# A graph kernel's attention: the row of s_dst through a DRAM line instead of TensorE transposes

## The chip, the cores and the metric

The kernel runs on one core of one Trainium2 chip. The metric is device time in microseconds (us), the median of the runs of a kernel. A profiled span is about 2 us shorter than the timed run (1584.6 against 1587.04 us before).

## The reference, cut to what matters

`x` is 64 x 256 x 128: 64 graphs of 256 nodes, 128 features each, all with one adjacency matrix. Four layers follow one another: a recurrent one (five steps), a masked graph convolution, an attention layer with an MLP, and a Chebyshev convolution. The change touches only the scores of the third layer.

```python
def _L2_gnn_ref(x, A_final, Wp, bp, a_src, a_dst, ...):
    h = jnp.einsum('bmi,ih->bmh', x, Wp) + bp
    s_src = jnp.einsum('bmh,h->bm', h, a_src)
    s_dst = jnp.einsum('bmh,h->bm', h, a_dst)
    scores = s_src[:, :, None] + s_dst[:, None, :]     # s_dst is needed as a row
    scores = jnp.where(scores >= 0, scores, 0.2 * scores)
    scores = jnp.where((A_final <= 0)[None], fill, scores)
    attn = jax.nn.softmax(scores, axis=-1)
    weighted_adj = attn * A_final[None]
    h_gat = jnp.einsum('bmn,bnh->bmh', weighted_adj, h)
    # ... layer norm, MLP, residual
```

## The kernel before

The batch is worked off as 32 pairs of graphs, each pair as four tiles of 128 tokens. Many pairs are in flight at once. A list scheduler inside the program decides, before anything runs, the order in which each engine's instructions stand. The scheduler plans with the costs that each `add` states, with one latency per engine (`SP` is the queue that issues nearly all transfers, 1383 of 1385), and with a place rule that says how far apart the pairs start.

```python
LATENCY = {PE: 230, ACT: 80, DVE: 80, POOL: 120, SP: 1800}

def place(p):
    return 20000 * min(p, 28)
# ... (cut)
        def turn(src, dst, view=lambda b: b.ap, tiles=4):    # transpose through DVE and 4 transfers
            S = flat("S") if tiles == 4 else big("S8")
            add(DVE, 705 if tiles == 4 else 1240,
                lambda: nc.vector.transpose(...), [src], [S], [S])
            def f():
                for k in range(4):
                    nc.sync.dma_start(dst.ap[:, :, 32 * k:32 * k + 32],
                                      S.ap[32 * k:32 * k + 32].rearrange("s (y r) -> s y r", r=32))
            add(SP, 2730, f, [S], [dst], [dst])
            return dst
# ... (cut) a recurrent step: mix (matmuls on htok), gates, the new state, and then
            h = turn(hT, wide("htok"))
# ... (cut) the attention; h2 holds h, s_src (column D) and s_dst (column D + 1)
        ts, sd = bank(), flat("sd")
        def f():
            for c in range(4):
                nc.tensor.transpose(ts.ap[:, c * P:(c + 1) * P],
                                    h2.ap[:, c, D + 1:D + 2].to_broadcast([P, P]), ident.ap)
        add(PE, 450, f, [h2, ident], [ts], [ts, sd])
        add(ACT, 585, lambda: nc.scalar.copy(sd.ap.rearrange("p (c x s) -> p c x s", x=4, s=32),
                                             ts.ap.rearrange("p (c s x) -> p c x s", x=4, s=32)), [ts], [sd])
# ... (cut) VectorE adds the mask to sd (tile u), softmax, turn(u) -> wT, matmul of wT with h
```

`htok` is the state of a pair by token: the result of each recurrent step, and the input of the next step's `mix`, brought to TensorE by four transfers of 64 KB on the SyncE queue.

## Time and profile before

| | before |
|---|---|
| time, median of the runs beside the changed kernel | 1587.35 us |
| span of the profiled execution | 1584.6 us |
| TensorE stream, summed from the matmul records | 1514.3 us |
| lost on TensorE: 100 to 1400 us / after 1400 us | under 7 us / 49.7 us |
| one pair, from its first matmul on wT to the next pair's | 47.1 us |

The stream is the sum of the distances from one matmul record to the next, each counted as at most the usual distance for its shape. "Lost" is time in which TensorE stands idle or runs at a lowered clock. First the windows view over the long middle; its columns are start and end, length, then busy us and instructions of TensorE, its weight loads, VectorE, ScalarE, GpSimd, then the granted clock, the DMA share and GB/s:

```profile
100.00:1400.00 1300.00, 1298.67 (x5384) 895.54 (x5384) 934.76 (x2059) 836.62 (x1883) 370.33 (x398) 1.00 0.44 77
```

TensorE is idle for 1300 - 1298.67 = 1.3 us in 1300. Second, the end of the view of the tile htok, how long its 640 transfers take from issue to landing:

```profile
DMA to landing us min/median/max: 2.3/2.4/3.9
```

They land in 2.4 us, none later than 3.9.

### The profile page before, as it was taken

The page shows a single profiled execution, that of the slowest core. Times are in us where ns is not written, and L with a number is a line of the kernel's source. Part 1 is how long each engine was busy: PE and PEld are TensorE (multiplying, and loading weights), DVE is VectorE, ACT ScalarE, POOL GpSimd, SP SyncE. Part 2 cuts the span into 40 slices and gives each one's busy share as a digit, 9 for nine tenths or more (in the row PEclk, how much of TensorE's full clock was granted, in tenths as well). Part 3 has the DMA queues.
Part 4 walks back from the last instruction along what each step waited for, and adds up shares of the span by engine and source line. Part 5 has one row for each costly group of instructions (what it writes and reads, how often), then busy time and mean ns, then how long its engine had stood idle before and what let it go on. Part 6 is the DMA issues. An engine that isn't in the chain of part 4 may idle for free.

```text
span 1584.6 us, 21441 instructions
## 1 busy us (share of the span) xinstructions
PE 1538.7 (97%) x6382; PEld 1070.4 (68%) x6382; DVE 1104.4 (70%) x2465; ACT 992.1 (63%) x2245; POOL 441.5 (28%) x487
## 2 busy tenths in 40 slices
PE   8999999999999999999999999999999999998767
PEld 5556667666677676667676667766767766676656
DVE  4687787667767677767676867776776766677553
ACT  3355676666666666666666666656666666677554
POOL 0001233332222323223323232233232231244441
PEclk9999999999999999999999999999999999999788
DMA  6223444444443444443444444344444344334422
GB/s 204 45 36 52 67 66 84 73 87 84 75 84 74 72 81 87 76 84 74 74 79 87 76 80 79 71 77 87 78 77 85 70 72 88 62 70 68 79 54 60
DMA packets 756611, 121.98 MB, mean 77 GB/s; under 512 B 743184, under 2 KB 743184, under 8 KB 756496
## 3 DMA queue, kind: packets, MB, share of 16 engines
q1 hardware_dynamic: 756208, 120.09, 42.1%
q8 instruction: 52, 0.85, 0.2%
q14 instruction: 63, 0.52, 0.1%
q10 hardware_dynamic: 288, 0.53, 0.1%
HBM read 19.86 MB, written 8.39 MB: 18 GB/s over the span
## 4 chain that ended last, share of the span: by engine, by line
PE 91%; DVE 2%; DMA 2%; ACT 2%; SPq 1%; issue 1%; POOL 1%; POOLq 0%; ACTq 0%; DVEq 0%
PE ps L513 27%; PE ps L607 9%; PE ps L589 9%; PE ps L597 8%; PE ps L605 8%; PE ps L592 8%; PE ps L740 7%; PE ps L526 6%; PE ps L702 4%; PE ps L749 3%; PE ps L647 2%; SPq L498 1%; PE ps L658 1%; DMA wT<-S 1%; DMA hT<-xT_in 1%
## 5 line engine op out<-in xcount | busy, mean ns | idle before, releaser
L516 ACT COPY mix<-ps 128x512 f32<-128x512 f32 x256 | 148.1, 580 | 197.7 <-PE ps L513 196.5
L513 PE MATMUL ps<-aTs,htok 128*128 128x256 f32 x1024 | 242.4, 380 | 2.8 <-DMA htok<-S 2.6
L513 PEld LDWEIGHTS ps<-aTs,htok 128*128 128x128 f32 x1024 | 192.6, 190 | 69.6 <-issue 32.8
L569 POOL TENSOR_SCALAR ss<-ss 128x4 f32<-128x4 f32 x96 | 38.2, 398 | 603.0 <-DVE ss L562 601.7
L611 DVE TENSOR_TENSOR hv<-hv,hT 128x512 f32<-128x512 f32 x160 | 124.2, 777 | 98.8 <-ACT hv L609 97.3
L570 POOL TENSOR_TENSOR rs<-ss,neg_half 128x4 f32<-128x4 f32 x128 | 139.2, 1087 | 192.0 <-DVE ss L564 183.8
L602 DVE SCALAR_TENSOR_TENSOR tr<-tr,hT 128x512 f32<-128x512 f32 x160 | 118.4, 742 | 91.4 <-ACT tr L595 91.3
L607 PE MATMUL ps<-tr,u5h 128*128 128x512 f32 x320 | 163.6, 594 | 0.4 <-DVE tr L602 0.2
L589 PE MATMUL ps<-hT,W 128*128 128x512 f32 x320 | 162.4, 593 | 1.1 <-DMA hT<-xT_in 1.1
L592 PE MATMUL ps<-mix,w4s 128*128 128x512 f32 x320 | 162.9, 593 | 0.0
L597 PE MATMUL ps<-mix,dw 128*128 128x512 f32 x320 | 162.8, 593 | 0.0
L605 PE MATMUL ps<-mix,w5s 128*128 128x512 f32 x320 | 162.6, 593 | 0.0
L609 ACT ACTIVATE hv<-ps,bh 128x512 f32<-128x512 f32 x160 | 109.4, 685 | 83.2 <-PE ps L607 80.6
L600 ACT ACTIVATE tz<-ps,bz 128x512 f32<-128x512 f32 x160 | 109.4, 685 | 60.0 <-PE ps L597 58.6
L595 ACT ACTIVATE tr<-ps,br 128x512 f32<-128x512 f32 x160 | 108.4, 679 | 39.3 <-PE ps L592 39.0
L612 DVE SCALAR_TENSOR_TENSOR hv<-tz,hv 128x512 f32<-128x512 f32 x160 | 108.9, 694 | 24.0 <-ACT tz L600 22.6
L562 DVE TENSOR_REDUCE ss<-sq 128x4 f32<-128x512 f32 x128 | 87.1, 681 | 48.1 <-ACT sq L559 48.1
L492 DVE STREAM_TRANSPOSE S<-hT 128x512 f32<-128x512 f32 x160 | 112.3, 703 | 1.1
L614 DVE SCALAR_TENSOR_TENSOR hT<-hv,hT 128x512 f32<-128x512 f32 x160 | 108.8, 693 | 4.9
L607 PEld LDWEIGHTS ps<-tr,u5h 128*128 128x128 f32 x320 | 60.4, 190 | 50.4 <-issue 36.4
L605 PEld LDWEIGHTS ps<-mix,w5s 128*128 128x128 f32 x320 | 58.6, 191 | 51.5 <-issue 31.1
L589 PEld LDWEIGHTS ps<-hT,W 128*128 128x128 f32 x320 | 58.3, 190 | 49.1 <-issue 42.8
(174 smaller groups left out, 2904.2 us busy)
## 6 DMA issues: line engine op xcount, KB each, us to landing
htok<-S SPq DMA_DIRECT2D x640, 64.0 KB, 2.4
xT<-S SPq DMA_DIRECT2D x256, 64.0 KB, 2.4
wT<-S SPq DMA_DIRECT2D x128, 128.0 KB, 3.8
xs<-xs_in SPq DMA_DIRECT2D x32, 256.0 KB, 2.8
hT<-xT_in SPq DMA_DIRECT2D x32, 256.0 KB, 3.0
dT<-S SPq DMA_DIRECT2D x128, 64.0 KB, 2.3
zT<-S SPq DMA_DIRECT2D x128, 64.0 KB, 2.4
y_out<-o SPq DMA_DIRECT2D x32, 256.0 KB, 2.0
```

The lines of the kernel that those rows point to most:

```text
L492: lambda: nc.vector.transpose(S.ap.rearrange("p (x c r) -> p x c r", x=4, c=tiles), view(src).rearrange("p (c x s) -> p x c s", x=4, c=til ...
L513: nc.tensor.matmul(t.ap[:, b * N:(b + 1) * N], src.ap[:, 2 * b + j, :], m.ap[:, j, :], start=(j == 0), stop=(j == 1))
L516: add(ACT, 590, lambda: nc.scalar.copy(o.ap, t.ap), [t], [o])
L570: nc.gpsimd.tensor_tensor(rs.ap, ss.ap, neg_half.ap, op=ALU.pow)
L589: add(PE, 865, lambda tg=tg: nc.tensor.matmul(tg.ap, mat("u3"), hT.ap, start=True, stop=False, skip_group_check=True), [hT, W0], [tg], [tg ...
L592: add(PE, 865, lambda tg=tg, mT=mT: nc.tensor.matmul(tg.ap, w4s.ap, mT.ap, start=False, stop=False, skip_group_check=True), [mT, w4s], [tg])
L597: add(PE, 865, lambda tg=tg, mT=mT: nc.tensor.matmul(tg.ap, dw.ap, mT.ap, start=False, stop=True, skip_group_check=True), [mT, dw], [tg])
L602: add(DVE, 735, lambda tr=tr: nc.vector.scalar_tensor_tensor(tr.ap, tr.ap, 1.0, hT.ap, op0=ALU.add, op1=ALU.mult), [hT], [tr])
L605: add(PE, 865, lambda tv=tv, mT=mT: nc.tensor.matmul(tv.ap, w5s.ap, mT.ap, start=True, stop=False), [mT, w5s], [tv], [tv, hv])
L607: add(PE, 865, lambda tv=tv, tr=tr: nc.tensor.matmul(tv.ap, u5h.ap, tr.ap, start=False, stop=True), [tr, u5h], [tv])
L611: add(DVE, 735, lambda hv=hv: nc.vector.tensor_sub(hv.ap, hv.ap, hT.ap), [hT], [hv])
L740: nc.tensor.matmul(tt[i].ap[:, b * N:(b + 1) * N], s, w.ap.rearrange("p k d -> p (k d)"), start=(b == 0 and k == 0), stop=False, skip_grou ...
```

## The change

Its intent is to take work from the busiest engine. Four transposes per pair leave TensorE and one copy leaves ScalarE. Instead, column D + 1 of h2 is written to a 2 KB line in DRAM (512 pieces of 4 bytes), and the line is read back into all 128 partitions. The row now has another order of nodes, so the mask addition, the transposing copy (`run=64`) and the order of one adjacency matrix follow it. The place rule changes too.

```diff
 def place(p):
-    return 20000 * min(p, 28)
+    return 24000 * min(p, 29)
@@ attention
-        ts, sd = bank(), flat("sd")
-        def f():
-            for c in range(4):
-                nc.tensor.transpose(ts.ap[:, c * P:(c + 1) * P], h2.ap[:, c, D + 1:D + 2].to_broadcast([P, P]), ident.ap)
-        add(PE, 450, f, [h2, ident], [ts], [ts, sd])
-        add(ACT, 585, lambda: nc.scalar.copy(...), [ts], [sd])
+        line, sd = Buf("line", 8, lambda i: dram.tile([1, 512], F32, tag=f"line{i}", name="line")), flat("sd")
+        add(SP, 650, lambda: nc.sync.dma_start(line.ap.rearrange("o (q s) -> s q o", s=32), h2.ap[:, :, D + 1:D + 2]),
+            [h2], [line], [line])
+        add(SP, 430, lambda: nc.sync.dma_start(sd.ap, line.ap.to_broadcast([P, 512])), [line], [sd], [sd])
@@ cut: mask addition on [p, 4, 64] views, turn(u, ..., run=64), host order of adjacency "as"
```

More of the change, by code (lines that the diff above doesn't have):

```diff
@@ L162 @@
     work = ctx.enter_context(tc.tile_pool(name="work", bufs=1))
+    dram = ctx.enter_context(tc.tile_pool(name="dram", bufs=1, space=bass.MemoryType.DRAM))
     psum = ctx.enter_context(tc.tile_pool(name="psum", bufs=1, space=bass.MemoryType.PSUM))
@@ L486, in add, with turn @@
             g.add(eng, cost, fn, (p, n[0]), reads, writes, takes)
-        def turn(src, dst, view=lambda b: b.ap, tiles=4):
+        def turn(src, dst, view=lambda b: b.ap, tiles=4, run=32):
             S = flat("S") if tiles == 4 else big("S8")
             add(DVE, 705 if tiles == 4 else 1240,
-                lambda: nc.vector.transpose(S.ap.rearrange("p (x c r) -> p x c r", x=4, c=tiles),
-                                            view(src).rearrange("p (c x s) -> p x c s", x=4, c=tiles)),
+                lambda: nc.vector.transpose(S.ap.rearrange("p (x c r) -> p x c r", x=4, r=run),
+                                            view(src).rearrange("p (c x s) -> p x c s", x=4, s=run)),
                 [src], [S], [S])
@@ L652, in build @@
                 hbias.ap[:, None, :].to_broadcast([P, 2, HW])), [t2, hbias], [h2])
-        ts, sd = bank(), flat("sd")
-        def f():
-            for c in range(4):
-                nc.tensor.transpose(ts.ap[:, c * P:(c + 1) * P], h2.ap[:, c, D + 1:D + 2].to_broadcast([P, P]), ident.ap)
-        add(PE, 450, f, [h2, ident], [ts], [ts, sd])
-        add(ACT, 585, lambda: nc.scalar.copy(sd.ap.rearrange("p (c x s) -> p c x s", x=4, s=32),
-                                             ts.ap.rearrange("p (c s x) -> p c x s", x=4, s=32)), [ts], [sd])
+        line, sd = Buf("line", 8, lambda i: dram.tile([1, 512], F32, tag=f"line{i}", name="line")), flat("sd")
+        add(SP, 650, lambda: nc.sync.dma_start(line.ap.rearrange("o (q s) -> s q o", s=32), h2.ap[:, :, D + 1:D + 2]),
+            [h2], [line], [line])
+        add(SP, 430, lambda: nc.sync.dma_start(sd.ap, line.ap.to_broadcast([P, 512])), [line], [sd], [sd])
         u = big("u")
@@ L671, in f @@
                 nc.vector.tensor_tensor_reduce(
-                    out=uc(c), in0=sd.ap[:, b * N:(b + 1) * N], in1=maskb.ap[:, it, :], scale=1.0,
+                    out=uc(c).rearrange("p (x f) -> p x f", x=4), in0=sd.ap.rearrange("p (x f) -> p x f", x=4)[:, :, 64 * b:64 * b + 64], in1=maskb.ap[:, it, :].rearrange("p (x f) -> p x f", x=4), scale=1.0,
                     scalar=-3.4e38, op0=ALU.add, op1=ALU.max, accum_out=mx.ap[:, c:c + 1])
@@ L692, in build @@
             a_s.ap.rearrange("p t j -> p (t j)")[:, None, :].to_broadcast([P, 2, 512])), [a_s], [u])
-        wT = turn(u, temp([P, 8, P], "w", N_W, "wT"), tiles=8)
+        wT = turn(u, temp([P, 8, P], "w", N_W, "wT"), tiles=8, run=64)
         add(DVE, 160, lambda: nc.vector.scalar_tensor_tensor(rd.ap, rd.ap, LN_EPS, rd.ap, op0=ALU.mult, op1=ALU.mult),
@@ L790 @@
     rows = [L1_gnn_bias, L2_gnn_bp, L2_gnn_gat_g, L2_gnn_gat_b, L2_gnn_b1, L2_gnn_b2, e[0, N - 1:], L2_gnn_eps]
-    adjs = {"a": adj, "as": adj[nodes], "ass": adj[nodes][:, nodes], "aTs": adj.T[nodes],
+    adjs = {"a": adj, "as": adj[nodes].reshape(N, 2, 4, 32).transpose(0, 2, 1, 3).reshape(N, N), "ass": adj[nodes][:, nodes], "aTs": adj.T[nodes],
             "aTss": adj.T[nodes][:, nodes]}
```

## The prediction

> **What bounds the kernel now.** I read the page's first two parts (busy shares, the 40 slices), then the chain of waits, then the busy time by window, then the groups of the lines that the change removes, then the timeline of one attention.
>
> ```profile
> PE 1538.7 (97%) x6382; PEld 1070.4 (68%) x6382; DVE 1104.4 (70%) x2465; ACT 992.1 (63%) x2245; POOL 441.5 (28%) x487
> ...
> PE   8999999999999999999999999999999999998767
> ...
> PEclk9999999999999999999999999999999999999788
> ...
> PE 91%; DVE 2%; DMA 2%; ACT 2%; SPq 1%; issue 1%; POOL 1%; POOLq 0%; ACTq 0%; DVEq 0%
> ```
>
> TensorE is busy to the nines until four slices from the end, and the chain that ended last is 91% TensorE. The other engines have a quarter or more of the span free. By window (length, then busy us and instructions of PE, PEld, DVE, ACT, POOL, then granted clock, DMA share, GB/s):
>
> ```profile
> 800.00:1000.00 200.00, 200.00 (x830) 137.87 (x829) 143.81 (x311) 132.37 (x302) 59.90 (x64) 1.00 0.45 78
> 1400.00:1450.00 50.00, 47.97 (x250) 37.34 (x249) 37.60 (x85) 38.02 (x96) 20.82 (x24) 1.00 0.47 78
> 1450.00:1500.00 50.00, 36.35 (x186) 30.49 (x184) 32.90 (x88) 34.40 (x93) 20.35 (x22) 0.86 0.44 69
> 1500.00:1550.00 50.00, 35.75 (x156) 30.22 (x157) 27.88 (x79) 29.12 (x76) 23.10 (x29) 0.80 0.29 51
> ```
>
> So there are two regimes. Up to about 1400 us TensorE never stops and its own stream sets the pace; the same attention matmul comes at 813.89, 861.03 and 908.17 us, one pair of the batch every 47.1 us, 32 pairs in all. After 1400 us the last pairs run out of company: TensorE waits, the granted clock falls to 0.80, and the length of one pair's chain of dependent work sets the end. From the starts of the matmul records I get 1514 us of pure streaming, about 6 us before the first matmul, 4 us of small gaps in the first 200 us, 1.5 us at 1318 us, 50 us lost after 1400 us (idle and slow clock) and 8 us after the last matmul: 1584 us. A timed run is about 2.4 us longer than the span (1587.04 against 1584.6).
>
> The removed part, over the whole run and in one pair:
>
> ```profile
> L658 PE MATMUL ps<-ident,h x128: 272/273/273, 139.6 to 1511.3; 128*128 128x128 f32 x128
> ...
> L660 ACT COPY sd<-ps x32: 579/586/592, 140.4 to 1511.6; 128x512 f32<-128x512 f32 x32
> ```
> ```profile
> 874.91 0.60 PE L658 MATMUL ps<-ident,h 128*128 128x128 f32 x4
> 875.54 0.59 ACT L660 COPY sd<-ps 128x512 f32<-128x512 f32 x1 [2.78 <-PE ps L658]
> 876.16 0.43 DVE L671 CUSTOM_DVE_ANT_0 u<-sd,maskb 128x256 f32<-128x256 f32 x1 [0.32 <-ACT sd L660]
> 892.65 3.61 SPq L498 DMA_DIRECT2D wT<-S  x4
> 908.17 1.95 PE L702 MATMUL ps<-h,wT 128*128 128x128 f32 x16
> ```
>
> A transpose's record lasts 273 ns, but that is latency: four start within 0.33 us, 0.11 us apart, and the chain puts 0.44 us on the four. The last wT transfer of this pair landed at 899.2 us and its matmul began at 908.2, so 9 us of waiting in the queue lie between the attention weights' arrival and their use.
>
> [...] The new write takes column D+1 of h2, so 512 elements of 4 B; the htok transfers of before also have 512 pieces (of 128 B), and land in 2.4 us. No transfer of before has 4-byte pieces. [...] here the y_out store lands 2.0 us after issue, so a DRAM target shows no penalty. [...] granted 1.00 while TensorE is full, 0.80 in the gappy tail. [...]
>
> **The change part by part.**
> Removed: 32 x 4 transposes x 0.111 us = 14.2 us of TensorE stream, 0.9% of the span. In the first regime all of it is on the path: a pair should take 47.14 - 0.44 = 46.7 us. Also 32 ACT copies x 0.586 = 18.8 us, on an engine 63% busy, so worth nothing there, and one use of a PSUM bank per pair.
> Added: 64 DMAs on the SyncE queue. Its 1280 transposing issues at 0.63 us (wT 0.79) take about 830 us, and it waits some 600 us, so another 64 x about 0.65 = 42 us fit. In the program's order four htok issues stand between the line's write and its read in nearly every pair of the first regime: 4 x 0.63 = 2.5 us, about the landing time of the write, so the read should block that in-order queue by a microsecond at most.
> The path of one pair: out go 0.44 (transposes) + 0.02 + 0.59 (copy), about 1.1 us. In come 0.65 issue + 2.4 landing (as htok) + 0.6 issue + 2.8 landing (as xs, also 256 KB out of DRAM) = 6.4 us, less about 0.8 because issues and landings overlap as they are counted. Net +4.5 us per attention.
> Moved: s_dst's order inside the row changes, and with it runs of 64 instead of 32 in the transposing copy and in the mask addition; element counts stay, so I count 0. The place rule (24000, 29 instead of 20000, 28) reorders everything. I listed both orders and summed the matmul streams between a pair's own matmuls. From h2's last matmul to the first one on wT: 36.1 us before, 39.0 after; the extra 3 us pay most of the 4.5, so some 7 us of the 9 remain and the detour is hidden. Elsewhere the new order is tighter (a pair lives 327 us of stream instead of 366), but the smallest distances, 12 us from the attention's matmul to the next mix and 14.7 us from u5h to the next mix, still exceed what those chains need in the trace (about 7.5 and 9.5 us).
> The tail: behind the last pair's first matmul stand 159 us of matmuls before and 179 after; behind the last matmul of its fifth recurrent step, 70 and 90. That last pair took from 1462.4 to 1577 us in the trace, 114.6 us for 70 us of stream: bound by its own chain. In the new order the same matmul should come at about 1421 x 0.992 (the streams I summed are 0.8% over the measured ones) + 6 + 4 + 1.5 + 5 of early tail gaps = 1427 us. Then 114.6 + 4.5 for the DRAM detour + 0 to 10, because now three pairs (not two) arrive there within 2 us of each other and queue for DVE, ACT and SyncE: last matmul at 1546 to 1556, span 1554 to 1564, timed 1556 to 1567.
> Sum: 14.2 us from the stream, about 12 us from a better filled tail: **1561 us**, 1.6% less.
>
> **The rivals.**
> (a) Only the stream counts and the tail loses its 50 us as before: 1587 - 14 = 1573. For: tail losses are stubborn, and the three pairs in step compete. Against: the last pair starts with 20 us more work behind it.
> (b) The SyncE queue becomes the bound: slow 4-byte writes (say 5 us) block it and htok comes late to matmuls in a fixed order. A stall of 1 us per pair would cost 32 us and give 1590. Against: the page's wait for DMA in the first regime is near 0, the distance at the attention is 39 us, and the recurrent steps have 5 us to spare.
> (c) The tail fills almost fully: streams 1500 + 6 + 4 + 2 + about 25 + 8 = 1545 span, 1548 timed. For: 114 - 90 = 25 us is the least that the last pair's chain leaves idle. Against: it needs no contention at all.
> (d) DMA load: 16384 pieces of 4 B are 2% more packets at a DMA share of 0.45; nothing.
>
> **Range and chances.** The first term is sure to a microsecond or two; the tail term may be -3 to +30. I take 1547 to 1576 for 8 in 10. Faster by over 2% means under 1555.3 us: 0.26. Slower by over 2% needs (b) in full: 0.03. Within 2%: 0.71.
>
> **What would show it.** The pair period in the middle 46.7 us and TensorE 200 of 200 us there; no L658 and L660 group; ACT's copy time down 19 us; the line's write landing in 2 to 3 us and sd's read in about 3; SyncE's wait on the line of a microsecond per pair; the matmul on wT not waiting for DMA before 1400 us; and the tail's loss after the last pair's fifth step about 35 us instead of 45. Wrong would be: TensorE gaps before 1300 us behind htok or wT, a landing of the line over 5 us, or a tail as long as before.

## The result, and the profile after

The changed kernel is correct, and slower.

| | before | after |
|---|---|---|
| time, median (range, runs) | 1587.35 us (1585.71 to 1587.93, 4) | 1687.38 us (1682.29 to 1695.21, 4) |
| span of the profiled execution | 1584.6 us | 1686.2 us |
| TensorE stream | 1514.3 us | 1500.3 us |
| TensorE idle, 100 to 1400 us | 1.3 us | 54.6 us |
| one pair in the middle | 47.1 us | 48.6 to 51.6 us |

The ratio is 1.0636, with a 95% interval of 1.0594 to 1.0678. Ratios here are the mean time of one kernel's fast runs over that of the other's fast runs of the same rounds, so they are not quite the ratio of the medians.

The stream fell by 14.0 us, close to the 14.2 predicted (13.3 if the usual distances are taken from the kernel before for both). The time rose by 100 us. First the page of the changed kernel: busy shares, slices, and the chain that ended last, by engine and by line.

```profile
PE 1555.9 (92%) x6254; PEld 1066.3 (63%) x6254; DVE 1127.9 (67%) x2465; ACT 983.6 (58%) x2213; POOL 426.9 (25%) x487
...
PE   8999999999999999999999999999999999996566
...
PE 63%; DMA 14%; DVE 13%; SPq 4%; issue 3%; ACT 2%; POOL 1%; ACTq 0%; DVEq 0%; POOLq 0%
PE ps L514 16%; DMA htok<-S 6%; PE ps L590 6%; PE ps L593 6%; PE ps L527 6%; PE ps L737 6%; PE ps L608 5%; PE ps L598 5%; PE ps L606 5%; SPq L499 4%; DMA line<-h 4%; PE ps L699 3%; PE ps L746 3%; DVE hv L613 3%; DMA sd<-line 2%
```

The slices still show nines, because a loss of 4% does not move a digit. The chain shows it at once: TensorE's share fell from 91% to 63%, DMA and VectorE took 27%. The largest transfer in it is not one of the two new ones but htok, which the change did not touch. The windows view, as before, has the middle and the end:

```profile
100.00:1400.00 1300.00, 1245.45 (x5027) 847.80 (x5026) 905.45 (x1950) 792.96 (x1780) 340.27 (x381) 0.99 0.47 78
...
800.00:1000.00 200.00, 192.42 (x790) 132.01 (x789) 138.72 (x299) 122.65 (x277) 54.15 (x61) 0.99 0.47 80
...
1500.00:1550.00 50.00, 34.26 (x150) 25.53 (x149) 30.23 (x84) 29.93 (x76) 16.64 (x19) 0.87 0.38 63
1550.00:1600.00 50.00, 31.81 (x154) 27.27 (x153) 24.93 (x69) 22.39 (x62) 11.96 (x16) 0.79 0.42 71
1600.00:1650.00 50.00, 30.04 (x162) 25.26 (x161) 26.19 (x55) 28.42 (x79) 24.30 (x28) 0.90 0.38 64
```

The stretch that was full (200.00 of 200) now has 192.42, and the other 200 us stretches from 200 to 1400 us have 189.72 to 193.30. Next, the transfers (KB each, median us to landing), and then the last line of the view of htok:

```profile
htok<-S SPq DMA_DIRECT2D x640, 64.0 KB, 2.4
...
sd<-line SPq DMA_DIRECT2D x32, 256.0 KB, 4.0
...
line<-h SPq DMA_DIRECT2D x32, 2.0 KB, 6.9
```
```profile
DMA to landing us min/median/max: 2.3/2.4/8.2
```

The write of 2 KB takes 6.9 us, longer than the 64 to 256 KB transfers of the steady state (medians of 2.3 to 4.0 us). The median of htok is unchanged, which hides what its maximum shows: 8.2 us instead of 3.9. I sorted the records: the 113 htok transfers issued within 4.5 us after a line write landed in a median of 6.0 us, the other 527 in 2.36. The waits view has who paid (us in total, times, longest us), first of the changed kernel:

```profile
DVE u L668 <- DMA sd<-line: 147.9, 31, 7.0
...
PE ps L514 <- DMA htok<-S: 43.6, 31, 2.9
```
```profile
SPq L658 <- DMA line<-h: 105.0, 30, 6.8
```

and then the one of them that the kernel before has too:

```profile
PE ps L513 <- DMA htok<-S: 2.6, 2, 1.3
```

There are three waits, each about once per pair: VectorE for the row, TensorE for htok, and SyncE's queue for the line. The timeline of SyncE's queue (start us, duration) shows one pair:

```profile
763.08 0.62 SPq L656 DMA_DIRECT2D line<-h  x1
763.79 2.66 SPq L499 DMA_DIRECT2D htok<-S  x4
769.38 0.33 SPq L658 DMA_DIRECT2D sd<-line  x1
```

The order is the one that the prediction counted on: write, four htok, read. The line landed at 769.32, and the four htok, issued between 763.79 and 765.82, landed at 769.49, 769.66, 769.83 and 771.48: the first three within half a microsecond after the line, none before it. The chain of waits, in order of time, shows what that did to TensorE in this pair and in the next:

```profile
765.82 5.66 DMA htok<-S
...
771.57 2.66 PE ps L514 x8
774.23 1.71 PE ps L590 x2
775.94 1.87 PE ps L514 x8
...
816.16 6.84 DMA htok<-S
...
823.14 3.03 PE ps L514 x8
```

The htok transfer lies on the chain with 5.66 us. TensorE stood for 2.06 us at 771.57. Then it was slow: eight mix matmuls took 2.66 us (1.73 elsewhere in the same chain), the next two 1.71 (0.86 elsewhere). The windows view in short stretches says why:

```profile
771.50:772.50 1.00, 0.93 (x4) 0.87 (x5) 0.00 (x0) 0.00 (x0) 0.00 (x0) 1.00 1.15 155
772.50:773.50 1.00, 1.00 (x4) 0.85 (x3) 0.00 (x0) 0.00 (x0) 0.00 (x0) 0.60 0.82 159
773.50:774.50 1.00, 1.00 (x3) 0.69 (x3) 0.71 (x5) 0.24 (x1) 0.00 (x0) 0.50 1.08 167
774.50:776.00 1.50, 1.50 (x3) 0.60 (x2) 1.43 (x9) 1.50 (x5) 0.00 (x0) 0.50 0.63 104
```

The granted clock fell to one half at 772.69 us for 3.41 us, 1.1 us after the end of the stall of 2.06 us. In the clock records of the changed kernel it did so nine times between 100 and 1400 us, for 3.41 us each, during a stall of TensorE or within 1.4 us after one; those nine stalls were 2.06 to 3.00 us long. One of 2.17 us (573.16 to 575.33) and all under 2 us left the clock at 1.00; why that one did, was not shown. So a stall that the waits view counts as 2.06 us costs about 2.06 + 0.93 + 0.85 + 0.14 = 4.0 us, most of the difference between the 46.7 us that were promised for a pair and the 51.1 that this one took. Over 100 to 1400 us the clock took 15.4 us in this way (the granted clock of 260 stretches of 5 us, summed), beside the 54.6 us of idleness: 70 us in the middle. In the kernel before, not one of those stretches was below 1.00. After 1400 us the changed kernel lost 86 us on TensorE, against 49.7 before, and that is most of the rest of the 100 us.

### The profile page after: what moved, and what is told of

It reads as the page before. It is cut to its first block, busy times and chain, and to the rows that moved or that the text cites. A ratio compares the mean times of both kernels' runs of the same rounds, so it can differ in the third digit from the quotient of the medians.

```text
span 1686.2 us, 21327 instructions
## 1 busy us (share of the span) xinstructions
PE 1555.9 (92%) x6254; PEld 1066.3 (63%) x6254; DVE 1127.9 (67%) x2465; ACT 983.6 (58%) x2213; POOL 426.9 (25%) x487
## 4 chain that ended last, share of the span: by engine, by line
PE 63%; DMA 14%; DVE 13%; SPq 4%; issue 3%; ACT 2%; POOL 1%; ACTq 0%; DVEq 0%; POOLq 0%
PE ps L514 16%; DMA htok<-S 6%; PE ps L590 6%; PE ps L593 6%; PE ps L527 6%; PE ps L737 6%; PE ps L608 5%; PE ps L598 5%; PE ps L606 5%; SPq L499 4%; DMA line<-h 4%; PE ps L699 3%; PE ps L746 3%; DVE hv L613 3%; DMA sd<-line 2%
## 5 line engine op out<-in xcount | busy, mean ns | idle before, releaser
L514 PE MATMUL ps<-aTs,htok 128*128 128x256 f32 x1024 | 252.3, 391 | 44.4 <-DMA htok<-S 43.6
L570 POOL TENSOR_SCALAR ss<-ss 128x4 f32<-128x4 f32 x96 | 21.1, 220 | 926.7 <-DVE ss L563 887.5
L612 DVE TENSOR_TENSOR hv<-hv,hT 128x512 f32<-128x512 f32 x160 | 110.3, 690 | 125.7 <-ACT hv L610 125.6
L590 PE MATMUL ps<-hT,W 128*128 128x512 f32 x320 | 165.8, 603 | 3.0 <-DMA hT<-xT_in 2.7
L571 POOL TENSOR_TENSOR rs<-ss,neg_half 128x4 f32<-128x4 f32 x128 | 133.2, 1041 | 69.7 <-DVE ss L565 45.9
L613 DVE SCALAR_TENSOR_TENSOR hv<-tz,hv 128x512 f32<-128x512 f32 x160 | 136.9, 857 | 20.7 <-ACT tz L601 19.2
L668 DVE CUSTOM_DVE_ANT_0 u<-sd,maskb 128x256 f32<-128x256 f32 x128 | 46.8, 422 | 147.9 <-DMA sd<-line 147.9
L603 DVE SCALAR_TENSOR_TENSOR tr<-tr,hT 128x512 f32<-128x512 f32 x160 | 108.5, 679 | 23.7 <-ACT tr L596 23.2
L678 ACT ACTIVATE u<-u,h 128x256 f32<-128x256 f32 x128 | 54.5, 496 | 100.0 <-DVE mx L668 100.0
```

The source lines that it names most:

```text
L514: nc.tensor.matmul(t.ap[:, b * N:(b + 1) * N], src.ap[:, 2 * b + j, :], m.ap[:, j, :], start=(j == 0), stop=(j == 1))
L571: nc.gpsimd.tensor_tensor(rs.ap, ss.ap, neg_half.ap, op=ALU.pow)
L590: add(PE, 865, lambda tg=tg: nc.tensor.matmul(tg.ap, mat("u3"), hT.ap, start=True, stop=False, skip_group_check=True), [hT, W0], [tg], [tg ...
L612: add(DVE, 735, lambda hv=hv: nc.vector.tensor_sub(hv.ap, hv.ap, hT.ap), [hT], [hv])
L613: add(DVE, 735, lambda hv=hv, tz=tz: nc.vector.scalar_tensor_tensor(hv.ap, tz.ap, 1.0, hv.ap, op0=ALU.add, op1=ALU.mult), [tz], [hv])
```

## The experiments

At hand were these theories. **Hold**: the write delays the completion of the transfers behind it. **Standing queue**: SyncE stands at the read until the line has landed, and everything behind it in the queue is issued late. **Late row**: VectorE stands at the mask addition for the row. **Order**: the new place rule is worse by itself. And for the write itself: is it slow for its number of pieces, their scattered order, their size, or its target?

All kernels, with what each left on TensorE in the middle. Idle is 1300 us less the busy time from 100 to 1400 us. W: values wrong. (1): one run only, state unknown.

| label | kernel | time us | ratio to before (95%) | idle us |
|---|---|---|---|---|
| | before | 1587 | 1 | 1.3 |
| | changed | 1687.4 | 1.0636 (1.0594 to 1.0678) | 54.6 |
| e3_no_write | W no write, row from a constant | 1593.6 | 1.0038 (1.0021 to 1.0054) | 2.9 |
| e4_write_not_read | W write, row from a constant | 1682.4 | 1.0588 (1.0568 to 1.0608) | 51.9 |
| e8_dve_no_wait | W all transfers, VectorE reads a constant | 1663.9 | 1.0499 (1.0468 to 1.0529) | 51.5 |
| e17_nobody_waits | W e4 and e8 together | 1648.8 | 1.0394 (1.0376 to 1.0412) | 43.7 |
| e18_write_from_act | W e4, write on ScalarE's queue | 1651.8 | 1.0417 (1.0398 to 1.0435) | 45.4 |
| e12_4B_to_sbuf | W e4, 512 x 4 B into SBUF | 1593.6 | 1.0040 (1.0023 to 1.0056) | 4.0 |
| e11_4B_in_order | 512 x 4 B in order of partitions | 1764.5 | 1.1113 (1.1094 to 1.1131) | 89.3 |
| e14_128_of_4B | W e4, 128 x 4 B | 1632.2 (1) | | 27.1 |
| e20_128_of_8B | W e4, 128 x 8 B | 1600.2 (1) | | 8.3 |
| e5_16B | 128 x 16 B | 1635.6 | 1.0288 (1.0266 to 1.0310) | 26.0 |
| e1_place_only | before, new place rule | 1608.8 | 1.0132 (1.0117 to 1.0147) | 5.3 |
| e2_old_place | changed, old place rule | 1776.3 | 1.1185 (1.1164 to 1.1206) | 105.8 |
| e15_dve_no_wait_old_place | W e8, old place rule | 1630.5 | 1.0271 (1.0254 to 1.0288) | 33.7 |
| e16_no_write_old_place | W e3, old place rule | 1619.3 | 1.0218 (1.0188 to 1.0248) | 29.6 |
| e7_latency | changed, scheduler told | 1619.9 | 1.0211 (1.0192 to 1.0230) | 23.4 |
| e10_16B_told | 16 B, told, old place rule | 1699.0 | 1.0702 (1.0686 to 1.0717) | 65.4 |
| e13_16B_replanned | 16 B, told, a third place rule | **1578.1** | 0.9945 (0.9930 to 0.9960) | 0.9 |

### Which part of the change costs the time

**e3_no_write.** The write is left out, and the row is read from a constant in DRAM of the same size. The order of the instructions is kept.

```diff
-        add(SP, 650, lambda: nc.sync.dma_start(line.ap.rearrange(...), h2.ap[:, :, D + 1:D + 2]), [h2], [line], [line])
-        add(SP, 430, lambda: nc.sync.dma_start(sd.ap, line.ap.to_broadcast([P, 512])), [line], [sd], [sd])
+        add(SP, 650, lambda: None, [h2], [line], [line])
+        add(SP, 430, lambda: nc.sync.dma_start(sd.ap, <512 constants of rows, to all partitions>), [line], [sd], [sd])
```

> The changed kernel with the write of the line left out and the row read from a constant input in DRAM (wrong values on purpose); every engine's order is that of the changed kernel. Theory A: the middle is full again, a pair every 46.7 us, and the time comes to 1555 to 1575 us. Theory B or theory C (the 256 KB read into every partition, or the load of the DMA rings): stays at 1660 us or more.

Measured: 1593.6 us, 94 us less than the changed kernel. In the middle the losses are gone (windows view):

```profile
100.00:1400.00 1300.00, 1297.08 (x5325) 890.72 (x5324) 959.71 (x2051) 841.66 (x1880) 362.27 (x402) 1.00 0.46 82
```

One pair takes 46.705 us, the 46.7 of the prediction. So the removal did what was promised, and reading 256 KB per pair, the strided VectorE forms and the new order cost the middle nothing. But the time is 33 us above the predicted 1561. It lies at the end: the last pair's fifth step came at 1430.0 us (predicted 1427), and from there the last matmul was 151.3 us away instead of the predicted 119 to 129. That second error is taken up under e1_place_only.

**e4_write_not_read.** The write is kept and the row comes from the constant, so SyncE does not stand at the read.

```diff
-        add(SP, 430, lambda: nc.sync.dma_start(sd.ap, line.ap.to_broadcast([P, 512])), [line], [sd], [sd])
+        add(SP, 430, lambda: nc.sync.dma_start(sd.ap, <512 constants of rows, to all partitions>), [line], [sd], [sd])
```

> The changed kernel with the write kept but the row read from a constant input, so that nothing waits for the write's landing (wrong values on purpose, same order). If the harm is only that SyncE and VectorE wait for the landing: as without the write, 1555 to 1575 us. If the write also holds up the transfers issued behind it (htok issued within 4.5 us after it landed in 6.0 us in place of 2.4): a good part of the loss stays, 1600 to 1650 us, and htok behind the write still lands in about 6 us.

Measured: 1682.4 us, only 5 less than the changed kernel and 89 more than without the write. Nobody uses what is written, and it still costs. Its transfers, in the order of that view:

```profile
sd<-rows_in SPq DMA_DIRECT2D x32, 256.0 KB, 5.5
...
line<-h SPq DMA_DIRECT2D x32, 2.0 KB, 7.1
```

The time is above both branches of the expectation. The htok transfers right behind a write landed in 6.2 us, though SyncE issued them without standing: line 749.42 to 756.09, htok issued from 750.14 on and landed at 756.26, 756.44, 756.61, 757.78. The read of the constant row, which has nothing to do with the line, takes 5.5 us instead of the 3.7 of e3_no_write, and VectorE waits 96.6 us for it instead of 37.2. The queue standing at the read falls as the main cause, the hold stands. (SyncE still waited 23.5 us in all for the line, before transfers that do not use it, L499. In the changed kernel's trace SyncE's 1447 issues share 8 semaphores, so a semaphore that is used again is the likely reason.)

**e8_dve_no_wait** and **e17_nobody_waits.** In the first all transfers are as changed, but VectorE adds the mask to a constant that is always there. The second does that and takes the row from the constant as well, so neither SyncE's read nor VectorE depends on the line.

```diff
-                    in0=sd.ap.rearrange(...)[:, :, 64 * b:64 * b + 64],
+                    in0=rbc.ap[:, :512].rearrange(...)[:, :, 64 * b:64 * b + 64],
```

> The changed kernel with both transfers and every order kept, but VectorE's addition reads a constant tile in place of the row (wrong values on purpose), so that no engine but SyncE waits for the row. If the loss goes through transfers held up behind the write (htok landing in 6 us): stays at 1670 us or more. If it goes mainly through VectorE standing still for the row (148 us in the trace): falls to 1600 to 1640 us.

> The changed kernel with the 4-byte write and a read of a constant row both issued, and nobody waiting for either (wrong values on purpose, same order). What is left above the 1594 us without a write is the hold on the transfers behind the write: 1640 to 1665 us if that is the main cause, below 1615 us if the waits for line and row are.

Measured: 1663.9 and 1648.8 us. With e3_no_write that makes a stair, each step a difference of medians: 1593.6 without the write; + 55.2 for a write that nobody waits for; + 15.1 when SyncE stands at the read; + 23.5 when VectorE waits for the row as well: 1687.4. In the other order, through e4_write_not_read, the last two steps are 33.6 for VectorE and 5.0 for SyncE, so those two cannot be parted sharply. The first step is the largest in either order. (1663.9 lies between the two branches of its expectation; 1648.8 is inside its first one.) The 33.6 us of VectorE in e4 belong to the hold as well: the row that VectorE waits for there is a constant, and e3, where it waits for the same constant, is the base of the stair. So 55 us is what the hold costs with nobody at the row, and 89 us what it costs with nobody needing the line. One limit: in e17 SyncE still waited 17.1 us for the line at the same place, L499, so "nobody waits" is not quite literal.

**e18_write_from_act.** As e4, but the write is issued on ScalarE's queue, while htok stays on SyncE's.

```diff
-        add(SP, 650, lambda: nc.sync.dma_start(line.ap.rearrange(...), h2.ap[:, :, D + 1:D + 2]), [h2], [line], [line])
+        add(SP, 650, lambda: nc.scalar.dma_start(line.ap.rearrange(...), h2.ap[:, :, D + 1:D + 2]), [h2], [line], [line])
```

> The kernel in which nothing reads the write (1682 us), with the write issued from ScalarE's queue in place of SyncE's. If the hold is in SyncE's own queue: htok issued within 4.5 us after the write lands in 2.4 us again and the time falls to 1590 to 1605 us. If it is in the DMA engines, across queues: htok behind it still takes about 6 us and the time stays at 1660 us or more.

Measured: 1651.8 us, between the two branches and 31 us below e4. The transfers view names the other queue:

```profile
line<-h ACTq DMA_DIRECT2D x32, 2.0 KB, 6.6
```

SyncE's waits for the line fell to 1.9 us in all, and htok behind a write still took 6.0 us. So the hold is not the order of one queue: a write of 6.6 us on ScalarE's queue holds htok on SyncE's. Where it sits was not shown. The semaphore records of the changed kernel show how closely the quick transfers follow the slow one. Each of these landings is counted in 16 steps; those of the line shown above came from 766.28 to 769.32 us, and those of the first htok behind it from 766.46 to 769.49, each 0.16 to 0.21 us after the line's. But it is not the notice alone that is late. In the records of the single pieces, 169 pieces of 128 bytes took over 1 us each between 100 and 1400 us of the changed kernel, the longest 3.3 us; in the kernel before, e3_no_write, e12_4B_to_sbuf, e20_128_of_8B and e5_16B not one took over 0.3 us. So part of the data of the quick transfers is held too. (The 31 us below e4 go with having the write off SyncE's queue; how, was not traced.)

### What makes the write slow

**e12_4B_to_sbuf.** As e4, but the same 512 pieces of 4 bytes go into an SBUF tile.

```diff
-        line, sd = Buf("line", 8, lambda i: dram.tile([1, 512], ...)), flat("sd")
+        line, sd = temp([P, 4, 2], "line", 8), flat("sd")
-        add(SP, 650, lambda: nc.sync.dma_start(line.ap.rearrange(...), h2.ap[:, :, D + 1:D + 2]), ...)
+        add(SP, 650, lambda: nc.sync.dma_start(line.ap[:, :, 0:1], h2.ap[:, :, D + 1:D + 2]), ...)
```

> As the experiment in which nothing reads the write (1682 us), but the 512 pieces of 4 B go to SBUF, each to its own partition, in place of DRAM (wrong values on purpose, same order). If 4 B pieces into DRAM are the cause: landing about 2.4 us, htok behind it no later than elsewhere, 1585 to 1600 us. If 4 B pieces are slow wherever they go: 1670 us or more.

Measured: 1593.6 us, exactly as without the write, and its line in the transfers view is:

```profile
line<-h SPq DMA_DIRECT2D x32, 2.0 KB, 2.0
```

Pieces, issues and queue are those of e4, and all 89 us are gone. The DRAM target is needed for the harm (landing in 7.1 us, here 2.0). It also clears the 32 extra issues of 0.6 us.

**e11_4B_in_order.** The pieces go to DRAM in the order of the partitions, 16 adjoining bytes from each, rather than scattered; a ScalarE copy sorts the row after the read.

```diff
-        ... line.ap.rearrange("o (q s) -> s q o", s=32) ...
+        ... line.ap.rearrange("o (p c) -> p c o", c=4) ...
+        add(ACT, 585, lambda: nc.scalar.copy(<sd in order>, <raw>), [raw], [sd])
```

> As the 16 B experiment (ScalarE puts the row in order), but without the gathering: 512 pieces of 4 B again, written to the line in the order of the partitions[...]. If the cost goes by the number of pieces: the landing stays at 6 to 7 us and the time is 1680 us or more. If it is the scattering over one another's DRAM lines: the landing falls to 2 to 3 us and the time to the 1636 us of the 16 B kernel, give or take 10.

Measured: 1764.5 us, values right; the write lands in 7.4 us, htok behind it in 6.2. The scattered order is not the cause. (The time suffers from the added copy in an order planned for none, so only the landing is used.)

**e14_128_of_4B** and **e20_128_of_8B.** As e4 with fewer pieces: 128 of 4 bytes (one of the four columns), or 128 of 8 bytes, gathered first by a VectorE copy.

```diff
# e14
+        ... line.ap.rearrange("o (c s x) -> s x c o", x=4, c=4)[:, :, 0, :], h2.ap[:, 0, D + 1:D + 2] ...
# e20
+        add(DVE, 160, lambda: nc.vector.tensor_copy(dcl.ap, h2.ap[:, :, D + 1]), [h2], [dcl], [dcl])
+        ... line.ap.rearrange("o (p c) -> p (o c)", c=4)[:, 0:2], dcl.ap[:, 0:2] ...
```

> As the experiment in which nothing reads the write, but only one of the four columns is written: 128 pieces of 4 B in place of 512 (wrong values on purpose). If the landing goes by the number of pieces put into DRAM: about 1.8 to 2.3 us, as with 128 pieces of 16 B, and the kernel at 1585 to 1605 us. If it is the size of 4 B: 6 us or more and over 1660 us.

> 128 pieces of 8 B in place of 128 of 4 B, gathered by VectorE first, read by nobody (wrong values on purpose). If 4 B alone is slow: landing about 1.8 us, htok behind it about 2.4 to 2.7 us, 1590 to 1610 us. If anything under 16 B is slow: landing 6 us or more and about 1630 us.

Measured, one run each: 1632.2 and 1600.2 us. The transfers view of the first, then of the second:

```profile
line<-h SPq DMA_DIRECT2D x32, 0.5 KB, 7.2
```
```profile
line<-dcl SPq DMA_DIRECT2D x32, 1.0 KB, 1.4
```

A quarter of the pieces takes as long as all of them (7.2 us, e4 7.1), so the number is not the cause. Twice the size per piece lands in 1.4 us, and htok behind it in 2.36, as if nothing stood before it. So pieces of 4 bytes in DRAM, as they lie here, do the harm (6.9 to 7.4 us in the changed kernel, e4, e11 and e14); pieces of 8 are free of it (1.4 us). Two things changed along with the size and were not tried alone: in e20 a VectorE copy gathers the source (e12 shows only that the strided source is harmless into SBUF), and its pieces start 16 bytes apart, while the 4-byte pieces of e14 and e11 adjoin. Whether 4-byte pieces that lie apart from all others are slow, no run shows. The expectation for e14 was right on the landing and wrong on the time (over 1660 us). Why e14 harms the time less than e4 at the same landing (htok behind it 4.8 us instead of 6.2) I did not settle.

**e5_16B.** A correct remedy: VectorE gathers the column to 128 x 4, the line is written in 128 pieces of 16 bytes, and ScalarE sorts the row after the read.

```diff
+        add(DVE, 160, lambda: nc.vector.tensor_copy(dcl.ap, h2.ap[:, :, D + 1]), [h2], [dcl], [dcl])
+        add(SP, 650, lambda: nc.sync.dma_start(line.ap.rearrange("o (p c) -> p (o c)", c=4), dcl.ap), [dcl], [line], [line])
+        add(SP, 430, lambda: nc.sync.dma_start(raw.ap, line.ap.to_broadcast([P, 512])), [line], [raw], [raw, sd])
+        add(ACT, 585, lambda: nc.scalar.copy(<sd in order>, <raw>), [raw], [sd])
```

> The changed kernel, right results, with the column first gathered by VectorE into a 128x4 tile, so that the line is written in 128 pieces of 16 B in place of 512 of 4 B, and a ScalarE copy that puts the row in order after the read. If the cost goes by the piece: the landing falls from 6.9 to about 3.4 us and the time to 1560 to 1600 us. If it is a fixed cost of a scattered store to DRAM: landing 6 us or more and 1660 us or more.

Measured: 1635.6 us, 52 less than the changed kernel. The line lands in 1.8 us (3.4 were expected) and htok behind it in 2.44, so the hold is gone. But the time misses the expected 1560 to 1600: TensorE is still idle for 26 us in the middle; the waits view has VectorE 49.5 us on the sorting copy, and the copy 36.4 us on the row. That points to the late row, an order planned for a row that comes sooner; it is argued, not shown, since e10 and e13 below change the place rule along with the plan.

### The order, and the end of the run

**e1_place_only.** The kernel before with the new place rule alone.

```diff
-    return 20000 * min(p, 28)
+    return 24000 * min(p, 29)
```

> The kernel before with nothing changed but the place rule (24000, 29). Theory A (the slow 4-byte write is the cause): the order is harmless, so 1570 to 1590 us, with TensorE 200 of 200 us busy in the middle and at best some 12 us off the tail. Theory B (the new, tighter order is the cause, a pair living 327 us of matmuls in place of 366): most of the 100 us appear here as well, 1640 us or more.

Measured: 1608.8 us, 21 more, between the two branches of the expectation. TensorE's idle time in the middle rose from 1.3 to 5.3 us, and the loss at the end from 50 to 65. The last three pairs ran their fifth step at 1443.0, 1443.9 and 1444.7 us (before: 1417.7, 1439.5, 1461.5), and from there it took 152.7 us to the last matmul, where the last pair of the kernel before took 114.5. So the place rule alone, with no DRAM line, makes that stretch 38 us longer. I summed the matmul records in it, by the usual distances: 69.8 us of stream before, 89.1 here and in e3_no_write. Half of the 38 us is thus more work left behind that point, and half (45 us lost before, 64 here, 62 in e3) more idleness and slow clock. That three pairs which run within 1.7 us of each other get in each other's way may account for the second half; it is argued, no run shows it alone.

**e2_old_place**, **e15_dve_no_wait_old_place** and **e16_no_write_old_place.** The changed kernel, e8 and e3, each with the old place rule.

```diff
-    return 24000 * min(p, 29)
+    return 20000 * min(p, 28)
```

> The changed kernel with the place rule of before (20000, 28). The place rule alone cost the kernel before 21 us. If that cost and the write's add up: 1660 to 1672 us. If the place rule made the stalls behind the write worse (less room between dependent work): below 1650 us. If it eased them: 1685 us or more.

> The changed kernel with the old place rule (1776 us), with VectorE's addition reading a constant tile in place of the row (wrong values on purpose). In that order few transfers stand right behind the write and VectorE waits 192 us for the row. If that wait is the cause of the extra 90 us: 1600 to 1660 us. If the hold is: 1720 us or more.

> The kernel without the write (1594 us) with the place rule of before (wrong values on purpose). If the new place rule is what spoils the tail, as it did in the kernel before (21 us): 1570 to 1580 us. If the tail is lost for another reason: 1588 us or more.

Measured: 1776.3, 1630.5 and 1619.3 us. The second is as expected. The first and the last are misses of mine: each falls into its open last branch, far beyond what I had in mind. In the order of the old rule only six htok stand right behind a write, but VectorE's waits for the row are longer (192.5 us in all, 10.7 the longest), and taking that wait away is worth 146 us. Even without the write that order loses 29.6 us in the middle, with VectorE waiting 58.7 us for a read of 3.6 us. So the place rule is not a sum with the rest: the new rule costs 21 us on the kernel before and saves 89 on the changed one. The order decides whose wait reaches TensorE.

**e7_latency**, **e10_16B_told** and **e13_16B_replanned.** Now the scheduler is told what the transfers take, through a latency per operation: in e7 for the changed kernel (6300 ns for the line, 3600 for the row), in e10 for the 16-byte form (1900 and 3700, and 1070 for the copy) with the old place rule, and in e13 as e10 with a third rule.

```diff
+    # add(..., lat=...): a latency for this operation, LATENCY[eng] where none is given
-            [h2], [line], [line])
+            [h2], [line], [line], lat=6300)                     # e7; in e10 and e13 [dcl], lat=1900
-        ... [line], [sd], [sd])
+        ... [line], [sd], [sd], lat=3600)                       # e7; in e10 and e13 [raw, sd], lat=3700
# place: e7 24000 * min(p, 29); e10 20000 * min(p, 28); e13 22000 * min(p, 29)
```

> The changed kernel, right results, with only the scheduler's figures corrected: it is told that the line lands 6.3 us after its issue and the row 3.6 us. If the loss is that the fixed order expected the row too early: 1580 to 1605 us. If the write holds up whatever is behind it, whenever that is: 1640 us or more, with htok behind the write still at about 6 us.

> The 16 B kernel (1636 us), right results, with the place rule of before and the scheduler told what the trace measured (line 1.9 us behind its issue, row 3.7 us, the reordering copy 1.07 us). If what was left of its loss is VectorE and TensorE waiting in a fixed order that was made for shorter waits: a pair every 46.7 to 46.9 us in the middle and 1565 to 1585 us, faster than the kernel before. If the two transfers load the rings anyway: a pair every 48 us as it was, 1610 us or more.

> The told 16 B kernel (1699 us) with another place rule (22000, 29), right results. If the 1699 us came from a poor order that the old place rule gave it, not from the transfers: a pair every 46.7 to 47.0 us in the middle and 1572 to 1592 us. If the transfers themselves cost: 1620 us or more, as with the other two orders.

Measured: 1619.9, 1699.0 and 1578.1 us. e7 lies between the two outcomes that I had set against each other: with the same slow write (7.0 us, htok behind it 5.5), an order that knows of it wins 67 us back. e10 is a plain miss: its write is quick and its scheduler informed, and it is slow, with TensorE waiting 52.4 us for htok; I did not trace why that order is poor. e13 differs from it only in the place rule and is 121 us quicker. Its middle, in the windows view, is full:

```profile
100.00:1400.00 1300.00, 1299.15 (x5340) 894.70 (x5339) 912.44 (x2098) 867.26 (x1910) 371.99 (x403) 1.00 0.46 83
```

One pair takes 46.705 us. e13 is correct and, at 1578.1 us (1572 to 1592 expected), 8.6 us below the kernel before in the same rounds and 109 below the changed one. The gain over the kernel before is small, 0.55%, but its interval leaves 1 out.

## Why the prediction was wrong

What held:

- **The stream.** Predicted -14.2 us; the records give 1514.3 - 1500.3 = 14.0 (13.3 by the stricter sum). The period of 46.7 us came as predicted wherever the slow write was away (e3, e13).
- **Forms and ScalarE.** The mask addition takes 422 ns in the mean (454 before), so the strided views cost nothing. The copy is gone, and nothing came of it.
- **The start of the end.** With the write away the last pair's fifth step was at 1430.0 us; 1427 was predicted (the terms of that sum give 1426).

What failed:

- **The landing of the line, and the rival that was turned down.** The step was "In come 0.65 issue + 2.4 landing (as htok)", and "the read should block that in-order queue by a microsecond at most". The 2.4 us were those of 128-byte pieces into SBUF, put on 4-byte pieces into DRAM. They took 6.9. The y_out store, which was to show that a DRAM target has no penalty, has pieces of 2 KB: the piece and the target were each looked at alone, and the harm needs both. For the pair shown above the detour was 10.7 us from the issue of the write (763.08) to the row's landing (773.77), against 6.4 less 0.8 in the working. The prediction had named "a landing of the line over 5 us" as what would prove it wrong, and its rival (b), slow 4-byte writes and late htok, as the way; it gave it 3%. So the danger was seen and misjudged, not missed.
- **The argument against the rival.** "The recurrent steps have 5 us to spare" looked at the distances of matmuls, and only for a queue that stands. The queue's standing at the read turned out to be the least of it (5 to 15 us). What was not thought of is that the slow write held the completion of transfers that were already issued, the four htok above all (a median of 6.0 us behind it, 2.36 elsewhere). They stand right behind it in the planned order, and the prediction itself counted on them to fill the wait. That hold is worth 55 us (e17 less e3) to 89 us (e4 less e3), in part through the lowered clock (granted 0.99 from 100 to 1400 us in e17 and e4, 1.00 in e3).
- **The end of the run.** The prediction took the 114.6 us of the last pair as "bound by its own chain" and added 4.5 and "0 to 10, because now three pairs (not two) arrive there within 2 us of each other". It had itself listed 70 and 90 us of matmuls behind that point, and counted the 20 more as free, filling what stood idle. In e3 the stretch took 151.3 us against 119 to 129: its 89.1 us of matmuls came as listed, but its loss was 62 us, where about 35 was predicted and 45 was there before. With 33 us more, 1561 becomes the 1594 that e3 measured, so with this order even a quick write would not have made the change quicker; with the order of e13_16B_replanned it did.

The sum: 1561 predicted, + 33 for the end, + 55 for the transfers held behind the write, + 38 for SyncE and VectorE waiting for line and row (a wait that e4 has for the most part with a constant row, held behind the write), is 1687. The parts were measured in kernels that differ from one another in one step each; that they add up is how they were formed, not a proof. Two small sums of the prediction are off and change nothing: a stall of 1 us per pair makes 1561 + 32 = 1593, not 1590, and 114 - 90 is 24. The chain shows the last term at the very end too:

```profile
1577.67 8.14 DMA line<-h
1586.77 6.98 DMA line<-h
1593.76 3.43 DMA sd<-line
```

Two writes stand one behind the other ahead of the last row: 18.6 us in the chain, in a stretch where no other work covers them.

What stays open: why a write of 4-byte pieces to DRAM takes over 5 us longer than one of 8-byte pieces (7.2 us in e14, 1.4 in e20; no run shows the mechanism), and whether their lying side by side is part of it; where the hold sits, since it reaches from one queue to another; what parts the longer end of the run between crowding and the pairs' own chains; and why the order of e10 is poor.

## What to carry to other kernels

Take a transfer's landing only from one with the same piece size and the same target (here 2.4 us were taken over from another and 6.9 came), and ask what is issued right behind it, for here a slow write also held quick transfers on another queue (e18: htok in 6.0 us behind a write of 6.6); gathering to 16 bytes per piece with one short VectorE copy removed this (e5: line in 1.8 us, htok in 2.44; with 8 bytes, in a single run, 1.4 and 2.36). Where an order is fixed beforehand, give the planner the measured latencies and try its spacing rule again, since the same rule cost 21 us on one version and saved 89 on another. Look at the maximum of a landing time and not only at its median (8.2 and 2.4 us for htok here), and count the lowered clock along with a stall (15.4 us here, beside 54.6 of idleness). When a better filled end is promised, add the work that is moved there.
